# Forming x W of eight row groups early and holding it in SBUF, in a graph layer on one Trainium2 core

## The chip, the cores and the metric

One core of one Trainium2 chip. The metric is the device time of one execution in microseconds (us); the median of several is given. Names of engines: PE is the tensor engine, DVE the vector engine, ACT the scalar engine, POOL GpSimd, SP the engine that only issues loads here.

## The reference

```python
HW = einsum('bnf,fo->bno', x, W)              # x: 8 x 4096 x 256, W: 256 x 256
A_norm = relu((A + A.T) * 0.5)                # A: 4096 x 4096, mostly zeros
D = sum(A_norm, axis=1)
d = where(D > 0, D ** -0.5, 0)
L = eye(N) - d[:, None] * A_norm * d[None, :]
y = layernorm(x + relu(einsum('nm,bmo->bno', L, HW)))
```

## The kernel before

It has two stages. The first walks over A in blocks of 512 x 512: it loads a block and its mirror, transposes on PE, adds on DVE, applies relu on ACT, sums rows for the degrees and stores the result in DRAM. A row group is 128 rows of the 4096; four of them make one block row, and their degrees are known when that block row is finished. A row group whose degrees are known can be projected: g = (x W) * d^-1/2, stored in DRAM. The second stage gathers, for each row group of the result, only those 128-wide pieces of A that hold something, with the rows of g that belong to them, and multiplies.

```python
        def project(m):
            xin = xpool.tile(...); nc.sync.dma_start(xin, x[rows m])
            xt = xpool.tile([P, B, FC, P], F32, tag="xt")         # pool of 2
            for b in range(0, B, 2):
                ... 4 transposes of xin into PSUM ...
                nc.scalar.copy(xt[:, b : b + 2], pt)
            g = xpool.tile([P, G], F32, tag="g")
            for b in range(0, B, 2):
                ... 4 matmuls of xt with W into pg ...
                nc.scalar.mul(g[:, b * FO : (b + 2) * FO], pg, r[:, m : m + 1])
            nc.scalar.dma_start(g_dram[m * P : (m + 1) * P, :], g)

        todo = []
        for i in range(NS):                                        # 8 block rows
            for j in range(i, NS):
                tij = load_adj(i, j); tji = load_adj(j, i) if j > i else tij
                symmetrise(i, j, tij, tji)
                if j > i: symmetrise(j, i, tji, tij)
                for _ in range(-(-len(todo) // (NS - j))):         # spread over the row
                    project(todo.pop(0))
            degrees(i)
            todo += range(i * A, (i + 1) * A)                      # four more are known
        ... lists for the first gathers ...
        for m in todo: project(m)
```

The second stage, for row group i of the result (cut; `xr` is loaded in `finish`):

```python
            py = [psum tile x 4]
            for t in range(CAP[i]):
                for c in range(4): nc.tensor.matmul(py[c], lhsT=at, rhs=gt[:, c*512:(c+1)*512], ...)
            gather(i + 1)                       # indirect loads on POOL, ten tiles deep
            nc.sync.dma_start(gself, g_dram[i * P : (i + 1) * P, :])
            finish(i, gself, py, ...)           # scale, relu, add x, layernorm, store
```

A scheduler orders the instructions of each engine when the program is built, so the order of the text is a wish and not the order that runs.

## Time and profile before

| what | value |
| --- | --- |
| time | 2015.96 us, median of 3 (2009.61 to 2018.54) |
| first stage, to the last scaled g | 592.6 us |
| join, from there to the first product | 18.4 us |
| second stage | 1401.3 us |
| projection of one row group on PE, alone | 1.75 + 6.91 = 8.66 us, 32 of them |
| row groups projected after the last block | 8 |

How to read it: in the first stage several engines take turns at being full, so a share of busy time over the whole stage says little. The useful cut is at the ends of the block rows, where the last add into a `sym` tile marks that a row of blocks is through.

### The profile page before, as it was taken

What the parts mean: (1) busy time and instruction counts of PE and PEld (TensorE: products, weight loads), DVE (VectorE), ACT (ScalarE), POOL (GpSimd) and SP (SyncE); (2) the same over time, 40 slices, a digit from 0 to 9 for tenths busy, and PEclk for the clock granted to TensorE, in tenths of its full rate; (3) what the DMA queues carried; (4) which work ended last, traced back from release to release, by engine and by line L of the source; (5) the groups of instructions that cost most, each with busy time, mean ns of one, the idle gap of its engine ahead of it and who ended that gap; (6) DMA issues with size and microseconds to landing.
All of it is one profiled execution on the core that took longest, in us unless ns stands there. A gap on an engine that the chain in (4) does not pass through costs nothing.

```text
span 2012.3 us, 18234 instructions
## 1 busy us (share of the span) xinstructions
PE 1832.4 (91%) x6720; PEld 1016.5 (51%) x6720; DVE 887.0 (44%) x1679; ACT 336.5 (17%) x353; POOL 918.9 (46%) x830
## 2 busy tenths in 40 slices
PE   5576777889978999999999999999999999999995
PEld 4465666778863444444444444444444444444442
DVE  6897989635100012243225323632642733342433
ACT  2334444546540000000000000000000000000000
POOL 0000000000006655586557766865666776666662
PEclk7688988989998999999999999999999999999998
DMA  9989998999859999999998999899899999999995
GB/s 372 395 316 374 332 380 294 404 373 338 269 203 406 404 362 363 366 327 398 383 379 319 399 410 399 333 409 411 314 399 407 353 411 411 412 412 412 413 409 196
DMA packets 245726, 738.08 MB, mean 367 GB/s; under 512 B 17136, under 2 KB 115744, under 8 KB 187520
## 3 DMA queue, kind: packets, MB, share of 16 engines
q0 software_dynamic: 68640, 434.55, 54.2%
q1 hardware_dynamic: 104960, 167.78, 23.3%
q10 hardware_dynamic: 72032, 134.51, 17.8%
q8 instruction: 56, 0.92, 0.2%
q14 instruction: 38, 0.31, 0.0%
HBM read 602.54 MB, written 134.24 MB: 366 GB/s over the span
## 4 chain that ended last, share of the span: by engine, by line
PE 62%; DMA 18%; DVE 13%; issue 4%; ACT 2%; POOL 1%; SPq 0%; DVEq 0%; POOLq 0%; ACTq 0%
PE py L354 51%; DMA gg<-g_dram,gi 10%; PE pg L248 8%; DMA a_dram<-sym 4%; DVE hot L147 3%; DVE sym L212 3%; DVE part L214 2%; DMA xin<-in_x_dram 2%; PE xtr L241 2%; PE tr L209 2%; ACT sym L213 2%; PE pl L167 1%; DVE stats L301 1%; DMA xr<-in_x_dram 1%; DVE y L296 1%
## 5 line engine op out<-in xcount | busy, mean ns | idle before, releaser
L354 PE MATMUL py<-gg,ga 128*128 128x512 f32 x3120 | 1364.1, 596 | 23.4 <-DMA xr<-in_x_dram 19.2
L354 PEld LDWEIGHTS py<-gg,ga 128*128 128x128 f32 x3120 | 585.0, 190 | 733.1 <-issue 729.2
L328 POOL DMA_INDIRECT ga<-a_dram,ai x390 | 424.6, 1089 | 305.2 <-PE py L354 145.0
L335 POOL DMA_INDIRECT gg<-g_dram,gi x390 | 415.3, 1065 | 224.2 <-DMA gg<-g_dram,gi 108.8
L295 ACT ACTIVATE y<-y,r 128x2048 f32<-128x2048 f32 x32 | 64.1, 2002 | 1337.9 <-DVE y L287 1259.0
L248 PE MATMUL pg<-w_sb,xt 128*128 128x256 f32 x1024 | 241.3, 392 | 20.7 <-ACT xt L242 20.4
L287 DVE SCALAR_TENSOR_TENSOR y<-gself,e,py 128x512 f32<-128x512 f32 x128 | 95.2, 747 | 372.2 <-PE py L354 364.5
L231 POOL TENSOR_TENSOR r<-e,neg_half 128x4 f32<-128x4 f32 x8 | 8.1, 1010 | 517.7 <-DVE e L230 517.7
L209 PE MATMUL tr<-ident,adj 128*128 128x128 f32 x1024 | 148.5, 308 | 96.4 <-DVE sym L212 73.5
L248 PEld LDWEIGHTS pg<-w_sb,xt 128*128 128x128 f32 x1024 | 196.3, 196 | 54.0 <-ACT xt L242 27.6
L212 DVE TENSOR_TENSOR sym<-tr,adj 128x512 f32<-128x512 f32 x256 | 158.9, 685 | 121.6 <-PE tr L209 98.5
L183 DVE TENSOR_SCALAR ai<-low 128x9 uint32<-128x9 f32 (+11 forms) x32 | 6.3, 198 | 425.8 <-DMA ga<-a_dram,ai 425.8
L209 PEld LDWEIGHTS tr<-ident,adj 128*128 128x128 f32 x1024 | 134.9, 161 | 108.8 <-DVE sym L212 83.5
L147 DVE TENSOR_TENSOR hot<-iota_q,at 128x4096 bf16<-128x4096 f32 x32 | 141.5, 4421 | 62.9 <-PE pl L167 62.9
L214 DVE TENSOR_REDUCE part<-sym 128x16 f32<-128x2048 f32 x64 | 144.8, 2280 | 14.3 <-ACT sym L213 14.2
L213 ACT ACTIVATE sym<-sym 128x2048 f32<-128x2048 f32 x64 | 122.4, 1912 | 148.1 <-DVE sym L212 126.2
L306 DVE TENSOR_SCALAR y<-y,mv,rstd 128x256 f32<-128x256 f32 x256 | 87.0, 412 | 51.0 <-POOL rstd L304 51.0
L255 ACT ACTIVATE gt<-pg,r 128x512 f32<-128x512 f32 x128 | 87.6, 689 | 114.5 <-PE pg L248 112.4
L301 DVE BATCH_NORM_STATS2 stats<-y 128x6 f32<-128x256 f32 x256 | 99.3, 402 | 0.9
L296 DVE TENSOR_TENSOR y<-y,xr 128x2048 f32<-128x2048 f32 x32 | 73.4, 2293 | 56.0 <-ACT y L295 47.6
L304 POOL TENSOR_TENSOR rstd<-rstd,neg_half 128x8 f32<-128x8 f32 x32 | 69.6, 2175 | 35.7 <-DVE rstd L303 35.1
L241 PE MATMUL xtr<-ident,xin 128*128 128x128 f32 x512 | 75.2, 303 | 3.9 <-DVE sym L212 3.3
(48 smaller groups left out, 369.8 us busy)
## 6 DMA issues: line engine op xcount, KB each, us to landing
adj<-in_adj_dram SPq DMA_DIRECT2D x64, 1024.0 KB
a_dram<-sym ACTq DMA_DIRECT2D x64, 1024.0 KB
xin<-in_x_dram SPq DMA_DIRECT2D x32, 1024.0 KB
g_dram<-gt ACTq DMA_DIRECT2D x32, 1024.0 KB
gself<-g_dram SPq DMA_DIRECT2D x32, 1024.0 KB
xr<-in_x_dram SPq DMA_DIRECT2D x32, 1024.0 KB
out_dram<-y ACTq DMA_DIRECT2D x32, 1024.0 KB
ga<-a_dram,ai POOLq DMA_INDIRECT x390
```

What stands on the lines that cost most here:

```text
L147: nc.vector.tensor_tensor(hot, iota_q.unsqueeze(1).to_broadcast([P, NB, P]), at[:, 1, k, :].unsqueeze(2).to_broadcast([P, NB, P]), ALU.is_ ...
L209: nc.tensor.transpose(pt[:, c * P : (c + 1) * P], tji[:, c, a * P : (a + 1) * P], ident)
L212: nc.vector.tensor_add(sym[:, a, :], pt, tij[:, a, :])
L213: nc.scalar.activation(sym, sym, AF.Relu, scale=0.5)
L214: nc.vector.tensor_reduce(part[:, i * A : (i + 1) * A, j * A : (j + 1) * A], sym.rearrange("p a (c q) -> p a c q", q=P), AX.X, ALU.add,)
L241: nc.tensor.transpose(pt[:, k, c, :], xin[:, b + k, c * P : (c + 1) * P], ident)
L248: nc.tensor.matmul(pg[:, k * FO : (k + 1) * FO], lhsT=xt[:, b + k, c, :], rhs=w_sb[:, c, :], start=(c == 0), stop=(c == FC - 1),)
L287: nc.vector.scalar_tensor_tensor(yf[:, c * S : (c + 1) * S], gself[:, c * S : (c + 1) * S], e[:, i : i + 1], py[c], ALU.mult, ALU.subtract,)
L301: nc.vector.bn_stats(stats[:, b, :], y[:, b, :])
L328: nc.gpsimd.indirect_dma_start(out=at, out_offset=None, in_=a_rows, in_offset=bass.IndirectOffsetOnAxis(ap=ai[:, t : t + 1], axis=0),)
L335: nc.gpsimd.indirect_dma_start(out=gt, out_offset=None, in_=g_dram, in_offset=bass.IndirectOffsetOnAxis(ap=gi[:, t : t + 1], axis=0),)
L354: nc.tensor.matmul(py[c], lhsT=at, rhs=gt[:, c * S : (c + 1) * S], start=(t == 0), stop=(t == CAP[i] - 1),)
```

## The change

The degrees of the last block rows come last, and PE then has eight projections to do with nothing beside them. The intent is to take the product x W, which needs no degrees, ahead: the last eight row groups are projected while the first block rows pass, their product stays in SBUF unscaled (8 KB per partition each), and when the degrees are there ACT scales the held tile in place and stores it. With that goes a new rule for the order: one projection behind every two blocks, known row groups first. To make room, adj goes from five buffers to four and xt from two to one.

```diff
-        tc.tile_pool(name="adj", bufs=5) as apool,
+        tc.tile_pool(name="adj", bufs=4) as apool,
+        tc.tile_pool(name="hold", bufs=HOLD) as hpool,          # HOLD = 8
...
-            xt = xpool.tile([P, B, FC, P], F32, tag="xt")
+            xt = xpool.tile([P, B, FC, P], F32, tag="xt", bufs=1)
...
-                nc.scalar.mul(g[...], pg, r[:, m : m + 1])
+                if known: nc.scalar.mul(to, pg, r[:, m : m + 1])
+                else:     nc.scalar.copy(to, pg)                 # to lies in a held tile
...
+        def release(m):
+            g = held.pop(m)
+            nc.scalar.mul(g, g, r[:, m : m + 1])
             nc.scalar.dma_start(g_dram[m * P : (m + 1) * P, :], g)
...
-                for _ in range(-(-len(todo) // (NS - j))):
-                    project(todo.pop(0))
+                credit += 1.0 if j > i else 0.5
+                while credit >= 1.0 and (known or early):
+                    form(known.pop(0), True) if known else form(early.pop(0), False)
+                    credit -= 1.0
+                credit = min(credit, 1.0)
...
+        for m in sorted(held): release(m)
```

More of the change, by code (lines that the diff above doesn't have):

```diff
@@ L51 @@
     G = B * FO
+    HOLD = 8
     EPS = 1e-5
@@ L231, in degrees, with form @@
             nc.gpsimd.tensor_tensor(r[:, ms], e[:, ms], neg_half[:, :A], ALU.pow)
-        def project(m):
+        held = {}
+        def form(m, known):
             xin = xpool.tile([P, B, F], F32, tag="xin", name=f"xin_{m}")
             nc.sync.dma_start(xin, x[:, m * P : (m + 1) * P, :].rearrange("b p f -> p b f"))
-            xt = xpool.tile([P, B, FC, P], F32, tag="xt", name=f"xt_{m}")
+            xt = xpool.tile([P, B, FC, P], F32, tag="xt", name=f"xt_{m}", bufs=1)
             for b in range(0, B, 2):
@@ L242, in project @@
                 nc.scalar.copy(xt[:, b : b + 2], pt)
-            g = xpool.tile([P, G], F32, tag="g", name=f"gt_{m}")
+            if known:
+                g = xpool.tile([P, G], F32, tag="g", name=f"gt_{m}")
+            else:
+                g = hpool.tile([P, G], F32, tag="held", name=f"held_{m}")
             for b in range(0, B, 2):
@@ L254, in project @@
                         )
-                nc.scalar.mul(g[:, b * FO : (b + 2) * FO], pg, r[:, m : m + 1])
+                to = g[:, b * FO : (b + 2) * FO]
+                if known:
+                    nc.scalar.mul(to, pg, r[:, m : m + 1])
+                else:
+                    nc.scalar.copy(to, pg)
+            if known:
+                nc.scalar.dma_start(g_dram[m * P : (m + 1) * P, :], g)
+            else:
+                held[m] = g
+        def release(m):
+            g = held.pop(m)
+            nc.scalar.mul(g, g, r[:, m : m + 1])
             nc.scalar.dma_start(g_dram[m * P : (m + 1) * P, :], g)
-        todo = []
+        known, early = [], list(range(NB - HOLD, NB))
+        credit = 0.0
         for i in range(NS):
-            pairs = NS - i
             for j in range(i, NS):
@@ L266 @@
                     symmetrise(j, i, tji, tij)
-                for _ in range(-(-len(todo) // (NS - j))):
-                    project(todo.pop(0))
+                credit += 1.0 if j > i else 0.5
+                while credit >= 1.0 and (known or early):
+                    if known:
+                        form(known.pop(0), True)
+                    else:
+                        form(early.pop(0), False)
+                    credit -= 1.0
+                credit = min(credit, 1.0)
             degrees(i)
-            todo += range(i * A, (i + 1) * A)
+            known += range(i * A, min((i + 1) * A, NB - HOLD))
+        for m in sorted(held):
+            release(m)
         ats = {}
@@ L276 @@
             make_list(i, ats[i // A])
-        for m in todo:
-            project(m)
+        for m in known:
+            form(m, True)
     def finish(i, gself, py, ypool, stat):
```

## The prediction

> **What bounds the kernel now.** I read the page's slices first, to find the stages. The tensor engine, the vector engine, the DMA engines and what they moved, in 40 slices of 50.3 us:
>
> ```profile
> PE   5576777889978999999999999999999999999995
> DVE  6897989635100012243225323632642733342433
> DMA  9989998999859999999998999899899999999995
> GB/s 372 395 316 374 332 380 294 404 373 338 269 203 406 404 362 363 366 327 398 383 379 319 399 410 399 333 409 411 314 399 407 353 411 411 412 412 412 413 409 196
> ```
>
> There are two programs end to end. The first twelve slices symmetrise A and form g = x W scaled; from slice thirteen on, gathered rows are multiplied and PE is at 90% or more in nearly every slice. The change touches only the first. Inside it the roles swap: DMA is full and PE half idle at the start, PE is full and DMA half idle in slices 11 and 12. That imbalance is what the change is after.
>
> Next I asked for the busy times by stage, with cuts where the trace shows a block row of A to end (the last add into its sym tiles). Columns: stretch, its length, busy time of PE, weight load, DVE, ACT, POOL, granted clock, DMA share, GB/s.
>
> ```profile
> 0.00:94.30 94.30, 49.12 (x258) 44.20 (x259) 68.74 (x80) 28.04 (x15) 1.34 (x10) 0.74 1.03 383
> 94.30:196.40 102.10, 73.14 (x534) 63.97 (x532) 90.35 (x115) 43.20 (x45) 1.03 (x1) 0.87 0.94 345
> 196.40:287.00 90.60, 68.50 (x497) 59.01 (x497) 78.37 (x101) 39.46 (x44) 1.01 (x1) 0.86 0.97 359
> 287.00:361.00 74.00, 60.67 (x405) 54.40 (x404) 65.39 (x78) 35.51 (x41) 1.01 (x1) 0.90 0.88 320
> 361.00:418.00 57.00, 44.37 (x255) 37.51 (x253) 33.10 (x40) 27.61 (x32) 1.01 (x1) 0.91 1.05 401
> 418.00:467.60 49.60, 46.37 (x272) 40.92 (x272) 24.26 (x31) 28.37 (x38) 1.01 (x1) 0.97 0.98 361
> 467.60:502.10 34.50, 32.01 (x192) 28.55 (x192) 14.61 (x19) 19.80 (x28) 1.01 (x1) 1.00 0.89 335
> 502.10:521.70 19.60, 19.10 (x110) 17.00 (x110) 7.51 (x10) 10.87 (x18) 1.01 (x1) 1.00 0.89 302
> 521.70:592.60 70.90, 68.25 (x373) 60.71 (x371) 2.91 (x4) 39.61 (x65) 1.01 (x1) 1.00 0.63 213
> 592.60:611.00 18.40, 0.00 (x0) 0.00 (x0) 0.00 (x0) 0.02 (x1) 8.79 (x9) 0.58 0.83 315
> ```
>
> Row 0 of blocks (to 94.3) is bound by DMA: share 1.03, PE 52% of the time. Rows 1 to 3 alternate between DVE, which there also makes gather lists (87 to 88% busy in all three), and DMA. Row 4 is DMA again (1.05). Rows 5 to 7 are PE: 93%, 93%, 97%. After 521.7 there is nothing but projection, eight row groups on PE at 96% with DMA at 213 GB/s. At 592.6 the last g goes out and PE stands still to 611.0.
>
> Last the chain of waits, at that join (start, length, what):
>
> ```profile
> 583.24 1.75 PE xtr L241 x16
> 584.98 6.92 PE pg L248 x32
> 591.93 0.69 ACT gt L255
> 592.64 3.86 DMA g_dram<-gt
> ...
> 597.48 13.39 DMA xr<-in_x_dram
> 611.08 102.33 PE py L354 x232
> ```
>
> A row group costs PE 1.75 + 6.91 = 8.66 us when it stands alone. Each of the eight after 521.7 lies on the path that sets the end. Then come the store (3.9), and 14.5 us until the first gathered rows are in, behind two xr and two gself loads that were queued ahead of them.
>
> **What the Trainium skill says.** "Perfetto Trace Analysis", Optimization Strategy, says that where the most-contended engine changes over time, interleaving the regimes may help. The table above is such a case. "DMA: Bandwidth & Descriptors", Issuing engines are not separate DMA queues, says DMAs started by different engines end up on the same 16 engines and interleave; the trace agrees, with a share of 1.03 to 1.05 where loads (issued by SP) and stores (issued by ACT) run together, at 383 to 401 GB/s. So an extra load in row 0 is not free. "TensorE: Matmul & The Clock Gate", Part 1, describes half clock after about 3.4 us of idleness; here a group of 16 transposes took 1.75 us at 583 us and 3.33 us at 94 us, where the engine had been waiting. The same page, Architectural detail, calls ACT a strict FIFO; the trace's ACT never overtakes, and I use that below.
>
> **The change, part by part.** The order of the built program matters more than the diff, so I compared the order of instructions on each engine.
>
> What moves: row groups 24 to 30 are projected one behind each of the seven block pairs of row 0, and 31 in row 1. Rows 2 to 4 keep four each. Row 5 has three (16 to 18) where it had four; row 6 has one (19) where it had four; behind the last block stand four (20 to 23) where there were eight. So eight projections, 8 x 8.66 = 69 us of PE, leave the stretch where PE binds. The rule "one per two blocks" does not empty the tail: after 31 the early ones are used up, rows 1 to 3 have no more known groups to offer, and credit is capped at one. I had first expected an empty tail; this order is why my figure is half the obvious one.
>
> What it costs in row 0: x for seven or eight groups, 1.05 MB each, in a stage where DMA is full. Before had two of these already loaded there (row groups 0 and 1), so six more: 6.3 MB / 0.39 MB per us = 16 us, less 2.7 us because one adj buffer fewer is prefetched, which only shifts that load. PE per pair becomes 3.5 (32 transposes at full clock, from the chain) + 8.66 = 12.2 us, measured 13.2 where pair and projection run together in row 5; DMA per pair is five MB-sized transfers, 5.24 MB / 0.39 = 13.4 us. Two limits this near to each other will not overlap perfectly, so I take 14.3 per pair. Row 0 ends at about 110, 16 us later.
>
> Rows 1 to 4: one x load more (2.7 us), and five adj buffers become four. A pair needs two, so loads are still one pair ahead, but less of the DMA's full stretches can be banked for the DVE stretches: I give 3 us. The end of row 4 goes from 418 to about 439. One xt buffer instead of two costs nothing: PE works in order, and the next group's copies come after its transposes, which stand behind the last read of xt.
>
> Rows 5 to 7: row 5 now needs ten A transfers and three each of x and g, 16.8 MB / 0.39 = 43 us, against 26 + 11 = 37 us of PE: DMA binds, 43 where it took 49.6. Row 6 moves 8.4 MB, 21.5 us, for 34.5. The last block stands behind group 19 and its copies on ACT: 12.5 us for 19.6. Sum 439 + 43 + 21.5 + 12.5 = 516 for 521.7 before. So up to here the change gains about 6 us only.
>
> The tail. Four groups instead of eight: 34.6 us instead of 69.3. Into it goes the new work on ACT. A scaling of a whole held row group is a 128x2048 activation, which the before kernel has with y at 2.0 us. Two stand behind row 6, and of the other six, one inside group 20 and five, 10 us, in one block ahead of xt of group 21; PE can transpose 21 into PSUM meanwhile but then waits. So the last g is scaled at 8.66 x 4 + 10 + the starting 2 = 46.5 us after the last add, for 70.9 before, and lands 4 us later. The eight held stores and what else is queued from row 6's end (about 19 MB, 48 us) are just done by then, so they are hidden.
>
> The join. The ten gathers of A now stand ahead of those of g and wait only for the held stores; they save about 1.5 us if early, cost 2 us if late. I leave 14.5 us. First product: 516 + 46.5 + 4 + 14.5 = 581, for 611.0.
>
> The second stage is the same instructions, 1401 us, with PE in the same state. Sum: 30 us less at most; with 1 us for a cold clock after the ACT wait, 29. 2015.96 - 29 = 1987 us, 1.4% faster.
>
> **The rivals.** (a) The full gain: the first stage becomes one balanced stretch. Its bytes in total (64 MiB in and out each for A, 32 each for x and g, 201 MB) at 0.4 MB per us are 503 us, so g could be complete at about 520 to 530, and the kernel at 1940 to 1950. For it: the slices with DMA at 5 and 8 tenths. Against: four projections still stand in the tail, and DVE holds DMA below 0.95 in rows 1 and 3, which nothing here changes. A milder form, where rows 5 to 7 run better than I think because DMA is ahead, gives 1970.
> (b) A new wait takes the gain: in row 0 the chain already passes through the stores of sym (three buffers, a store of 9.3 to 10.4 us each). If x loads stretch these stores to 13 us, PE waits for DVE, DVE for a sym buffer, and with four adj buffers loads then start late. A pair at 16 to 17 us would eat another 10 to 15 us: 2000.
> (c) Nothing moves, because the second stage's gathers are limited by the DMA: after an earlier start they run at the same 379 GB/s, so the start is passed on in full. I see no way for that stage to give it back; PE lists only 23 us of waiting there, 19 of them at the join.
> (d) Slower than before would need row 0 and the lost buffer to cost 60 us. Row 0 has 45 us of idle PE, so no.
>
> **Range and chances.** The terms that I trust least are row 0 (+16, could be +10 to +30), the buffer (0 to +10) and rows 5 to 7 (a gain of 27 us against before, could be 15 to 35). Taken together that is some 13 us either way as a standard deviation, so eighty in a hundred lie from 1968 to 2004. Two per cent is 1975.6, 11 us below my figure: faster 0.2, within two per cent 0.78, slower 0.02.
>
> **What would show it.** Row 0 ends at 105 to 115 with a DMA share above 1; row 4 at 435 to 445; last add into sym at 510 to 522; ACT shows eight 128x2048 activations of held at 2.0 us, five of them in a row with PE idle some 8 to 10 us just then; four projections after it; g complete near 567, first product near 581; 1401 us from there to the end. I am wrong if row 0 takes its x loads without getting longer (then the gain is near 45), if row 4 ends after 450 (then near 15), or if the second stage changes its length.

## The result, and the profile after

The changed kernel took 1982.68 us, median of 4 (1978.11 to 1987.96); the kernel before, with the runs made beside it, 2013.26 (median of 4). The ratio is 0.9847, 95% interval 0.9809 to 0.9885: the same within 2%, and 1.5% faster. Ratios here are the mean time of one kernel's fast runs over the mean of the other's of the same rounds, so they are not quite the ratios of the medians.

The same table by stage, of the changed kernel, cut where its own block rows end (stretch, length, busy PE, weight load, DVE, ACT, POOL, granted clock, DMA share, GB/s). The last three lines are the tail, the join and the second stage:

```profile
0.00:107.80 107.80, 88.56 (x544) 79.01 (x544) 66.35 (x79) 54.06 (x64) 1.35 (x10) 0.95 1.01 367
107.80:216.60 108.80, 89.15 (x630) 79.16 (x630) 90.78 (x115) 51.24 (x60) 1.03 (x1) 0.94 0.96 354
216.60:308.80 92.20, 66.49 (x497) 57.74 (x497) 80.66 (x102) 39.48 (x43) 1.01 (x1) 0.88 0.96 357
308.80:383.10 74.30, 59.11 (x405) 53.11 (x404) 65.38 (x78) 35.54 (x41) 1.01 (x1) 0.89 0.89 325
383.10:434.10 51.00, 43.21 (x255) 37.67 (x253) 33.35 (x40) 27.77 (x32) 1.01 (x1) 0.93 1.05 397
434.10:481.80 47.70, 40.38 (x224) 34.77 (x224) 24.18 (x31) 23.56 (x30) 1.01 (x1) 0.89 1.02 381
481.80:499.70 17.90, 15.00 (x96) 12.91 (x96) 14.49 (x20) 9.96 (x11) 1.01 (x1) 1.00 1.04 405
499.70:514.30 14.60, 11.58 (x61) 10.30 (x62) 7.39 (x9) 10.22 (x11) 1.01 (x1) 0.88 1.06 411
514.30:563.80 49.50, 35.70 (x181) 30.91 (x179) 2.90 (x4) 32.23 (x39) 10.79 (x11) 0.90 0.77 299
563.80:580.00 16.20, 1.52 (x2) 0.83 (x3) 0.00 (x0) 0.00 (x0) 8.57 (x9) 0.60 0.81 311
580.00:1978.20 1398.20, 1369.17 (x3833) 610.36 (x3831) 501.92 (x1210) 64.05 (x32) 891.11 (x793) 0.99 0.97 380
```

PE's work in row 0 went from 49 to 89 us, and the row became 13.5 us longer. In rows 5 to 7 the DMA is now full (share 1.02 to 1.06), where PE had been; in row 4 it was so before (1.05). The tail is 49.5 us long but PE is busy in only 35.7 of them.

| stage | before, us | changed, us | difference |
| --- | --- | --- | --- |
| block row 0 | 94.3 | 107.8 | +13.5 |
| rows 1 to 3 | 266.7 | 275.3 | +8.6 |
| row 4 | 57.0 | 51.0 | -6.0 |
| rows 5 to 7 | 103.7 | 80.2 | -23.5 |
| tail, last add to last scaled g | 70.9 | 49.5 | -21.4 |
| join, to the first product | 18.4 | 14.7 | -3.7 |
| second stage | 1401.3 | 1399.7 | -1.6 |
| span of the profiled run | 2012.3 | 1978.2 | -34.1 |

The chain of waits through the changed kernel's tail (start, length, what):

```profile
514.32 1.91 ACT sym L216
...
516.76 7.19 PE pg L257 x32
...
524.56 2.00 ACT held L276
...
533.16 2.00 ACT held L276
...
536.18 8.95 PE pg L257 x32
545.13 1.75 PE xtr L247 x16
...
562.45 16.02 issue
578.48 21.95 PE py L384 x44
```

Group 20 is multiplied from 516.8 to 524.0. Then ACT scales five held tiles in a row, 524.6 to 535.2, and only then copies xt of group 21, which PE waits for. Group 21 takes 8.95 us where a warm group takes 6.91: the granted clock is 0.50 from 529.6 to 539.8 us. "issue" at 562.45 covers the store of the last g, its landing and the first gather; PE does nothing in it.

### The profile page after: what moved, and what is told of

It is laid out like the page before. It is cut to its first block, busy times and chain, and to the rows that moved or that the text cites. A ratio compares the mean times of both kernels' runs of the same rounds, so it can differ in the third digit from the quotient of the medians.

```text
span 1978.2 us, 18260 instructions
## 1 busy us (share of the span) xinstructions
PE 1819.9 (92%) x6720; PEld 1006.8 (51%) x6720; DVE 887.4 (45%) x1679; ACT 348.1 (18%) x361; POOL 918.9 (46%) x830
## 4 chain that ended last, share of the span: by engine, by line
PE 68%; DMA 13%; DVE 11%; issue 4%; ACT 3%; POOL 1%; SPq 0%; ACTq 0%; POOLq 0%; DVEq 0%
PE py L384 54%; PE pg L257 8%; DMA gg<-g_dram,gi 7%; PE tr L212 3%; DVE hot L149 3%; DMA a_dram<-sym 2%; DVE sym L215 2%; DMA adj<-in_adj_dram 2%; PE xtr L247 2%; DVE part L217 1%; ACT sym L216 1%; DMA xin<-in_x_dram 1%; PE pl L169 1%; DVE stats L331 1%; DVE y L326 1%
## 5 line engine op out<-in xcount | busy, mean ns | idle before, releaser
L384 PE MATMUL py<-gg,ga 128*128 128x512 f32 x3120 | 1363.6, 596 | 18.4 <-issue 16.0
L257 PE MATMUL pg<-w_sb,xt 128*128 128x256 f32 x1024 | 247.6, 398 | 38.2 <-ACT xt L248 38.1
L212 PE MATMUL tr<-ident,adj 128*128 128x128 f32 x1024 | 132.1, 289 | 58.5 <-DVE sym L215 34.6
L212 PEld LDWEIGHTS tr<-ident,adj 128*128 128x128 f32 x1024 | 123.7, 150 | 65.9 <-DVE sym L215 40.3
L334 POOL TENSOR_TENSOR rstd<-rstd,neg_half 128x8 f32<-128x8 f32 x32 | 69.5, 2173 | 42.2 <-DVE rstd L333 41.6
L248 ACT COPY xt<-xtr 128x512 f32<-128x512 f32 x128 | 69.8, 582 | 62.1 <-PE xtr L247 50.9
```

The source lines that it names most:

```text
L212: nc.tensor.transpose(pt[:, c * P : (c + 1) * P], tji[:, c, a * P : (a + 1) * P], ident)
L257: nc.tensor.matmul(pg[:, k * FO : (k + 1) * FO], lhsT=xt[:, b + k, c, :], rhs=w_sb[:, c, :], start=(c == 0), stop=(c == FC - 1),)
L384: nc.tensor.matmul(py[c], lhsT=at, rhs=gt[:, c * S : (c + 1) * S], start=(t == 0), stop=(t == CAP[i] - 1),)
```

## The experiments

Where ends of block rows, the tail or the join are given below, they are read from the trace of the run's profiled execution, as in the table. All kernels but the two called wrong matched the reference.

### 1. The rule without the holding

```diff
-    HOLD = 8
+    HOLD = 0
```

> The change's order rule (at most one projection per two blocks, credit capped at one, four adj buffers, one xt) without any row group formed early. My theory: the holding is what pays, and the rule alone only pushes projections from block rows 5 and 6 into the tail, which becomes 12 projections (104 us) after a last add at about 500 us; last g scaled near 606 instead of 592.6, kernel 10 to 15 us slower than before, ratio 1.005 to 1.008. Rival: the even spreading itself is what pays; then this kernel is faster than before, ratio 0.995 or less.

Measured: 2020.95 us, ratio 1.0064 (1.0047 to 1.0081): slower. Last add at 496.0, tail of 12 projections 105.6 us, last g scaled at 601.6. So the holding is what pays. This kernel is also the right one to count from, since it differs from the changed one in the eight row groups alone. Against it the changed kernel reaches the last add 18.3 us later (514.3), has a tail 56.1 us shorter (49.5), a join 3.5 us shorter and a second stage 1.1 us longer: 40.2 us faster in the profiled runs. Eight projections taken from the tail are 8 x 8.66 = 69 us; 13 of these are lost in the tail itself and 18 are paid for earlier.

### 2. The buffers alone

```diff
-        tc.tile_pool(name="adj", bufs=5) as apool,        # in the kernel before
+        tc.tile_pool(name="adj", bufs=4) as apool,
-            xt = xpool.tile(..., tag="xt")
+            xt = xpool.tile(..., tag="xt", bufs=1)
```

> The kernel before with only the two buffer cuts (adj 5 to 4, xt 2 to 1). My theory: 0 to 5 us, ratio 1.000 to 1.0025, block row 4 ends at 418 to 423. Rival: the lost prefetch costs 10 us or more (ratio over 1.005), and the change's gain would be that much larger if the memory were there.

Measured: 2013.56 us against 2009.35, ratio 1.0023 (1.0007 to 1.0040), about 4.6 us. Its profiled run ended row 4 at 415.1 (418.0 before), so the trace doesn't show a place where the loss falls. The cost is small and within what I had set down for it.

### 3 and 4. What lengthens block row 0

My prediction had row 0 at about 110 us because of the x loads. Two kernels with a wrong result take the two possible causes away in turn. The first multiplies one of four pairs of batches and copies that to all of the held tile; the second loads x once for seven early groups.

```diff
-            for b in range(0, B, 2):                      # light_pe, transposes and matmuls
+            for b in range(0, B if known else 2, 2):
...
-            nc.sync.dma_start(xin, x[rows m])             # no_x_load, groups 25 to 30
+            xin = first[0]                                # the tile of group 24
```

> Wrong result on purpose: the eight early row groups load all their x and fill all of their held tile on ACT, but PE transposes and multiplies only one of the four pairs of batches (2.2 us instead of 8.7). Theory of two equal limits: the DMA bound of block row 0 lies at the same place as PE's, so row 0 still ends at 104 to 110 us. Rival, PE and ACT alone set row 0 now (13.3 us per pair, PE 82% busy): row 0 ends at 100 us or before, near the 94 us of the kernel before.

> Wrong result on purpose: the projections of row groups 25 to 30 use the x of group 24, so six loads of 1.05 MB leave block row 0 while PE and ACT do the same work. If the chain of PE and ACT sets the 13.3 us per pair, row 0 still ends at 105 to 109 us. If the DMA sets it, row 0 ends 10 to 16 us earlier, at 92 to 98 us.

Measured, end of row 0: 98.2 us with little PE work, 105.6 without the loads; 107.8 in the changed kernel, 93.7 with no early groups. So six loads are worth at most 2 us and three quarters of PE's work 9.6. The 2 us may be nothing: runs below with the same order in row 0 and all loads ended it between 105.6 and 107.4 us (experiments 5, 6 and 8 to 11). The chain in row 0 of the changed kernel, one pair of blocks:

```profile
62.53 3.49 PE tr L212 x32
66.03 1.32 PE xtr L247 x12
67.35 0.57 ACT xt L248
67.94 1.91 ACT sym L216
69.85 0.48 ACT xt L248
70.38 5.45 PE pg L257 x24
```

It repeats every 13.3 us, is PE's for 10.3 of them, and no DMA is in it. The other 3 us are ACT's: at 67.94 it takes the relu of the block (1.91 us) between two copies of xt, and PE waits for the second copy. The same part of the run with little PE work:

```profile
47.06 16.68 DMA adj<-in_adj_dram
63.73 0.14 issue
63.87 1.96 PE tr L212 x8
65.82 0.02 issue
65.85 1.89 DVE sym L215 x3
```

There it is the load of A that ends last, and the row needs 98 us with the loads of x for the early groups in it. At the end of row 4 that run stands at 418.3 us, where the kernel without any early groups stands at 418.9: the loads of x cost nothing by then, and the 15 us that the changed kernel pays come with the work on PE and its copies on ACT. Without the six loads row 4 ends at 434.9, no earlier than with them (434.1). The light run also spares ACT three of four copies of xt, so the two runs show PE and the copies that feed it, not PE alone. Each is one profiled execution in an unknown state.

### 5. The scaling on VectorE

```diff
-            nc.scalar.mul(g, g, r[:, m : m + 1])
+            nc.vector.tensor_scalar(g, g, r[:, m : m + 1], None, ALU.mult)
```

> The changed kernel with the eight held tiles scaled by VectorE instead of ACT, and nothing else. My theory: the block of scalings on ACT, ahead of the copies of group 21, is what keeps PE idle for 10.5 us in the tail and cools its clock; with it gone the last g is scaled 38 to 40 us after the last add into sym (49.5 in the changed kernel), kernel 9 to 12 us faster than the changed one, ratio to before 0.978 to 0.981. Rival: the wait is replaced by another, the stores of the held tiles reach the DMA later or collide with the last groups' stores and the gathers wait for them: less than 4 us gained, ratio 0.983 or more.

Measured: 1977.98 us, ratio 0.9835 (0.9820 to 0.9850), against 0.9847 for the changed kernel. The two intervals overlap, so in time no gain is shown. The tail is 45.6 us and not 38 to 40. The expectation failed, and the rival's number (0.983 or more) came true. From the timeline of that run (start, length, engine, what, idle time before it and what ended it):

```profile
528.12 0.33 ACTq L277 DMA_DIRECT2D g_dram<-held  x1
528.77 0.33 ACTq L270 DMA_DIRECT2D g_dram<-gt  x1
529.19 3.84 ACTq L277 DMA_DIRECT2D g_dram<-held  x3
533.07 2.05 ACT L248 COPY xt<-xtr 128x512 f32<-128x512 f32 x4 [4.33 <-DMA g_dram<-held]
533.71 10.19 PE L257 MATMUL pg<-w_sb,xt 128*128 128x256 f32 x32 [3.94 <-ACT xt L248]
```

DVE scaled four tiles in 4.9 us while PE worked, as it should. But ACT still issues their stores (ACTq is its queue). Five issues stand ahead of the copies of xt; the last three took 1.14 to 1.27 us each, where one mostly takes 0.33, and they fill the time to 533.03. The copy follows 0.04 us later. The profile infers that the landing of a held store ended ACT's 4.33 us, but between the last three issues there is no gap of more than 0.1 us in which ACT could have waited for a landing: it was issuing. Why the three took so long no run shows. PE's gap shrank from 10.5 to 3.9 us and did not close, and group 21 ran cold for 10.19 us. One wait had taken the place of the other.

### 6. The four loads at the join

The four loads gself 0 and 1 and xr 0 and 1 are made to wait for the tenth gather by a small copy into their tiles that reads it.

```diff
+            if i < 2:
+                nc.vector.tensor_copy(gself[:, 0:1], tenth[:, 0:1])     # and the same for xr
             nc.sync.dma_start(gself, g_dram[i * P : (i + 1) * P, :])
```

> The changed kernel, with the two xr and two gself loads that stand ahead of the first gathers made to wait until the tenth gather of g has landed. If these four loads (4.2 MB, 10 us at 0.41 MB per us) are what the first product waits for, it starts 4 to 7 us after the last g has landed instead of 10.6, kernel 4 to 6 us faster than the changed one. Rival: the latency of the software gathers themselves sets it: 0 to 2 us gained.

Measured: 1976.09 us, ratio 0.9828 (0.9813 to 0.9844). The last g was scaled at 562.7 and the first product came at 573.0, 10.3 us later, against 14.7 in the changed kernel. The gain is 4.4 us at the join, and the theory holds: the first product now comes 6.4 us after the last g has landed, within the 4 to 7 expected. By the ratios alone the two kernels are not told apart.

### 7. Another dealing of the early groups

```diff
-                credit += 1.0 if j > i else 0.5
-                while credit >= 1.0 and (known or early):
+                credit = min(credit + (1.0 if j > i else 0.5), 1.5)
+                while credit >= 1.0 and (known or (early and (i > 0 or j % 2 == 0))):
```

> The changed kernel with the early row groups dealt out differently: three in block row 0, three in row 1, two in row 2; the tail has four as before. Theory after the last two runs: in row 0 it is PE's and ACT's chain that each early group lengthens (by 1.8 us each, 13.3 against 11.5 per pair), not the DMA, so row 0 ends at 99 to 102 us; rows 1 and 2 have 20 and 26 us of idle PE and take five groups for 0 to 3 us each in all: last add into sym 2 to 8 us earlier than in the changed kernel. Rival: rows 1 and 2 are full where the groups go (their ends are bound by the DMA after the lists), so what row 0 gains is lost there: last add within 2 us of the changed kernel's 514.

Measured: 1986.36 us, ratio 0.9885 (0.9867 to 0.9904), by the ratio a little slower than the changed kernel, though the intervals just meet. Row 0 ended at 104.5, later than expected for three groups in it. Row 1 ended 9 us earlier than in the changed kernel, row 4 only 2 us earlier, and the last add came at 513.2 against 514.3. The rival's number came true. Of the 9 us, 3.7 were lost in row 2 and 3.4 in row 4. Row 4 ran at a DMA share of 1.05 and 406 GB/s there, but PE had one group more to do in it (304 PE instructions for 255), and which of the two took the time back was not tested. The time itself was lost in the tail, 54.8 us: in this order seven of the eight scalings on ACT stand behind the last block, from 515 to 530 us.

### 8. No cap on the credit

```diff
-                credit = min(credit, 1.0)
```

with the scaling on VectorE.

> The scaling on VectorE, and credit not capped at one, so that rows 5 and 6 take four and three projections again and one stands behind the last block instead of four. If only the sum of PE work from row 5 on counts, nothing is gained over the scaling on VectorE alone: the last add comes 24 to 30 us later and the tail is that much shorter, kernel within 4 us of it. Rival (the tail is long because the cap put four projections there): 8 us or more faster than with the scaling on VectorE alone. A third outcome, slower by 5 us or more, would say that the held stores, with no projections left to hide them, end up on the path.

Measured: 2016.14 us, ratio 1.0018 (1.0000 to 1.0037), 38 us slower than with the cap. Of my three outcomes the third (slower by 5 us or more) came true, but its reason covers only a part: against experiment 5 the first product comes 15 us later after the last scaling (30.8 us for 16.0), while the last add comes 57 us later, where I expected 24 to 30, for a tail that is 33 us shorter. The theory that only the sum of PE work counts has fallen. Without the cap unused credit piles up while no group is known; when four become known, all four are projected one after the other at the start of the next row. Rows 3, 4 and 5 of that run:

```profile
314.90:407.40 92.50, 64.36 (x404) 56.05 (x403) 67.63 (x79) 35.99 (x41) 1.01 (x1) 0.83 0.83 300
407.40:475.20 67.80, 54.64 (x305) 48.60 (x305) 32.97 (x41) 32.17 (x39) 1.01 (x1) 0.85 0.94 335
475.20:535.30 60.10, 47.10 (x275) 41.14 (x274) 23.84 (x31) 28.37 (x37) 1.01 (x1) 0.93 0.92 334
```

They do the work of the changed kernel's rows 3 to 5 (74.3, 51.0 and 47.7 us), with one group more in each of rows 4 and 5 (305 and 275 PE instructions for 255 and 224), at a lower DMA share. Two groups are 17 us of PE; the three rows took 47 us more. For 35 us at a time PE lets no block of A pass; with four adj buffers the loads then have nowhere to go, which fits the lower share, though no run took that apart. In the end the eight held stores stood behind everything; the last landed at 601.9 us and the first product came at 616.6. "One row group per two blocks" is therefore a working part of the change, not a nicety.

### 9. Held stores from another queue

```diff
-            nc.scalar.dma_start(g_dram[m * P : (m + 1) * P, :], g)
+            nc.gpsimd.dma_start(g_dram[m * P : (m + 1) * P, :], g)     # in release, on top of 5
```

> The scaling on VectorE again, and the stores of the held tiles issued from GpSimd's queue instead of ACT's. Theory: in the run with only the scaling moved, ACT still stood 4.3 us before the copies of group 21 because the stores that it issues wait for earlier DMAs to land; with the issue gone from ACT, group 21 follows group 20 without a gap, PE stays warm, and the last g is scaled 36 to 39 us after the last add (45.6 there, 49.5 in the changed kernel); ratio to before 0.977 to 0.981. Rival: the tail is held by the DMA, which has some 19 MB to move from row 6's end: then the last g is scaled early but lands 8 us or more after (4 to 6 so far), or the held stores land after it, and the kernel is within 3 us of the changed one.

Measured: 1974.92 us, ratio 0.9826 (0.9808 to 0.9844). PE in the tail:

```profile
517.42 8.86 PE L257 MATMUL pg<-w_sb,xt 128*128 128x256 f32 x32 [1.94 <-ACT xt L248]
526.11 1.91 PE L247 MATMUL xtr<-ident,xin 128*128 128x128 f32 x16
527.86 7.07 PE L257 MATMUL pg<-w_sb,xt 128*128 128x256 f32 x32
534.77 1.91 PE L247 MATMUL xtr<-ident,xin 128*128 128x128 f32 x16
536.52 7.07 PE L257 MATMUL pg<-w_sb,xt 128*128 128x256 f32 x32
546.96 1.94 PE L247 MATMUL xtr<-ident,xin 128*128 128x128 f32 x16 [3.37 <-DMA xin<-in_x_dram]
```

Groups 20, 21 and 22 follow each other without a gap and the two after 20 run warm. So the stores on ACT's queue were what held group 21 in experiment 5; that they waited for landings, as I had expected, is not shown. The tail is 41.6 us, not 36 to 39, and the ratio is outside what I expected and not told apart from experiment 5: PE then stood 3.4 us for the x of the last group, whose load ran beside the stores. The rival, the DMA as the limit of the tail, may begin there; the sign that I had set for it did not come (the last g landed 4.1 us after its scaling, not 8).

### 10 and 11. The parts together

Nine groups held (g from the same ten buffers), with 5, 6 and 9; and the same with a whole credit for diagonal blocks from row 5 on.

```diff
-                credit += 1.0 if j > i else 0.5
+                credit += 1.0 if j > i or i > 4 else 0.5          # 11 only
```

> Scaling on VectorE, held stores from GpSimd's queue, the four loads of the join made to wait for the tenth gather, and nine held row groups (the tiles of g taken from the same ten buffers), so three projections in the tail. Theory: the parts add up: tail 28 to 31 us from the last add to the last scaling, join 6 us from landing to the first product, first product at 553 to 562 us (578.5 in the changed kernel), ratio to before 0.970 to 0.976. Rival: held stores from a software queue delay the first gathers or r, which stand on the same engine: first product later than 565.

> As the combination, and from row 5 on a diagonal block counts a whole credit, so group 19 stands behind the diagonal block of row 6, group 20 behind the last pair and 21 and 22 behind the last block; never more than one at a time. PE has 3 us to spare in each of rows 6 and 7 and 7 in row 5: theory, last add 4 to 12 us later than in the combination, tail 8.7 us shorter, kernel within 4 us of the combination either way. Rival (the bunching that cost 38 us with the cap off begins here too): 8 us or more slower.

Measured: 1967.10 us, ratio 0.9781 (0.9762 to 0.9800), and 1958.64 us, ratio 0.9747 (0.9734 to 0.9761). The second is the fastest kernel, 2.5% faster than before and about 1% faster than the change as it was. The first missed its expectation: first product at 568.1 and not 553 to 562, because PE waited for the x of a late group; its chain of waits holds one load of x that took 29.3 us, from 513.8 to 543.1, and PE stood 11.7 us for it. The rival's number (later than 565) came true; whether the held stores delayed that load was not tested. The second was expected within 4 us of the first and was 8 us faster. Row 6 and the tail of the second:

```profile
477.30:503.20 25.90, 23.35 (x144) 20.77 (x144) 15.95 (x20) 15.15 (x19) 1.77 (x2) 1.00 1.05 408
...
516.70:538.80 22.10, 17.71 (x80) 14.88 (x80) 7.78 (x8) 11.46 (x17) 3.89 (x5) 0.92 1.02 424
```

One group moved from the tail (three there in experiment 10, two in 11) into row 6, and the last add came only 3.5 us later. The tail is 20.3 us shorter, 22.1 for 42.4: 8.7 of these are the group, and most of the rest is PE's wait for x, down from 11.7 to 1.2 us. Why that wait went was not taken apart. The join's gain of experiment 6 is not in these two (12.6 and 16.4 us): the first gathers of A, issued early in the changed kernel, here alternate with those of g behind the last store. From row 4 to the end of the tail the DMA share is now 1.02 or more.

### 12. One pair earlier

The projection is called ahead of `symmetrise` instead of behind it.

> The last combination, with each projection called ahead of its block pair instead of behind it, so that every group stands one pair earlier on PE and only group 22 stands behind the last block (two there before: 21 and 22). Theory: from row 4 on that kernel keeps the DMA full (share 1.02 to 1.05 to the end of the tail), so PE work taken from its tail no longer counts: first product within 4 us of its 555.2, ratio to before 0.973 to 0.977. Rival: the tail is still PE's, and 8.7 us less of it are 6 to 9 us gained, ratio 0.970 to 0.972. Third outcome: group 23 ahead of the first pair delays the whole of row 0 by a load and a projection, 5 us or more slower.

Measured: 1972.61 us, ratio 0.9811 (0.9799 to 0.9824), 14 us slower. Row 0 ended 7.2 us later (112.8), and row 4 21.6 us later (452.9). The third outcome is what came, with more than its 5 us. Row 0 explains a third; why row 3 and row 4 then took 12 and 5 us longer was not tested, so whether the tail of experiment 11 is bound by the DMA alone stays open.

## Why the prediction was right or wrong

**The total was right**: 1987 predicted, 1982.68 measured, 29 us of gain against 31 between the medians. Two of its terms, row 0 and rows 1 to 4, had about the right size for a partly wrong reason. That the sum is so close is partly luck: against the forecast, row 0 and rows 1 to 4 together came 5 us short, rows 5 to 7 and the tail 6 us long and the join 4 us short.

**What moves** was right. The order of the built program showed four projections left behind the last block, and that halved the obvious figure. The trace has four there.

**Row 0, +16 us to about 110**: 107.8. The size holds, the reason failed. The prediction put it on x loads into a full DMA ("6.3 MB / 0.39 MB per us = 16 us"). Experiments 3 and 4 show at most 2 us for six loads and 9.6 for three quarters of PE's work and its copies. A DMA share of 1.03 did not mean that six more megabytes could not be moved in the time. I had PE's 13.2 us per pair in hand, from row 5, and named it a second limit near the first; that chain, PE with ACT's copies and relu, was the one that bound, at 13.3.

**Buffers and rows 1 to 4, end at 439**: 434.1. For the buffers I gave 3 us, measured in the kernel before as 4.6 with an interval from 1.4 to 8. Rows 1 to 3 took 8.6 us more than before, where I gave 5.7, and row 4, which I left at 57, took 51; why was not tested.

**Rows 5 to 7, 77 us**: 80.2 (47.7, 17.9 and 14.6 for 43, 21.5 and 12.5). That DMA takes the place of PE as the bound there held: share 1.02 to 1.06.

**The tail, 46.5 us**: 49.5. The wait behind the scalings was predicted at 8 to 10 us and was 10.5. What I had set too low is the cold clock after it: group 21 needed 8.95 us for 6.91. "TensorE: Matmul & The Clock Gate", Part 1, says half clock after about 3.4 us of idleness, and the trace agrees in kind here and in experiment 5 (10.19 us after 3.9 us of waiting). But group 20 in experiments 5 and 9 also took 8.86 us, after a wait of only 1.94 (granted clock 0.50 from 519.4 to 522.7 in experiment 5), so a shorter wait met the half clock too.

**The join, 18.5 us from last scaling to first product**: 14.7. The gathers of A, which wait only for the held stores, were issued from 547 us on and were out of the way; I had allowed them 1.5 us. That they are the whole difference is read from the order, not tested.

**The second stage** was right: 1399.7 us against 1401.3.

**The rivals.** That the stores of sym take over did not come true: DVE waited 8.6 us in all for them up to the last add, 22.8 in the kernel before. That everything balances did not come true in this version, for the reasons that the prediction gave, nor did its milder form (rows 5 to 7 took 80.2 us, more than the 77 forecast); experiment 11 shows that one per cent more was to be had (ratio 0.9747 for 0.9847). That the second stage passes an earlier start on in full held in every run, with lengths from 1397 to 1401 us.

## What to carry to other kernels

Work moved out of the stretch where its engine binds pays once, less what it lengthens where it lands and what its new steps (here the scalings on ACT, and their stores) put ahead of the work that the binding engine waits for; look for the latter in the built order before the run. A full share of DMA is no proof that one more load costs its bytes: take away the loads and the work in turn, and see which one moves the end. And deal moved work out evenly: here up to four projections in a row went with a lower DMA share, and that kernel lost 38 us, more than the whole change had gained.

## What the Trainium skill lacked or had wrong

- "DMA: Bandwidth & Descriptors", Issuing engines are not separate DMA queues, says that issuing from several engines saves only the issue time of a sequencer, usually small next to the DMA. It does not say that this time stands ahead of the compute of the issuing engine, or that it can grow: in experiment 5 three issues in a row took ACT 1.14 to 1.27 us each, where one mostly takes 0.33, and the copies that PE waited for came only after them; with the eight stores on GpSimd's queue the tail was 41.6 us instead of 45.6.
- "Perfetto Trace Analysis", Optimization Strategy, advises to interleave regimes with different bounds, and this change agrees with it (ratio 0.9847). It lacks that the grain decides: the same work, four at a time instead of one, gave 1.0018 with the scaling on VectorE, where one at a time gave 0.9835.
- "Perfetto Trace Analysis", Identifying the Most-Contended Engine, warns that occupancy of the DMA engines misleads. The runs agree, and it was my reading of the share that went against it; what the page lacks is a test. At a share of 1.01 and 367 GB/s row 0 was not bound by the DMA: without six loads the share fell to 0.90 and the row ended at 105.6 instead of 107.8 us, a time that experiment 11 also reached with all its loads.
